# Where four short transposes stand in TensorE's order: among the projections, or behind the values of two blocks

## The chip, the cores and the metric

The kernel runs on one core of one Trainium2 chip. The time is device microseconds (us) from start to end of one execution; of several runs the median counts. An execution recorded by the hardware profiler gives the trace from which all durations here are taken.

## What is computed

Two transformer blocks, one after the other, work in float32 on `x` of 8 batches, 512 tokens and width 256. The change touches block 0 alone. Cut to its core it is:

```python
def _L0_xcond_ref(x, c, brain_tokens, ...):           # H = 16 heads of width 16
    h = modulate(ln(x), shift_sa, scale_sa)
    q = ln(_heads(h, H)) * qn_w + qn_b
    k = ln(_heads(h, H)) * kn_w + kn_b
    v = _heads(h, H)
    attn = softmax(einsum('bhqd,bhkd->bhqk', q, k) * scale)
    x = x + gate_sa * _unheads(einsum('bhqk,bhkd->bhqd', attn, v))
    h = modulate(ln(x), shift_ca, scale_ca)           # cross-attention over 64 context tokens
    ...
    x = x + gate_ca * h
    h = modulate(ln(x), shift_ff, scale_ff)
    h = silu(h @ w1.T) * (h @ w3.T) @ w2.T
    return x + gate_ff * h
```

Block 1 (self-attention with rotary positions, cross-attention, a GELU layer) follows with heads of width 64.

## The kernel before, in words

**Blocks of scores and values.** Self-attention of a batch is cut into four head groups `g` of four heads, and each into four key tiles `kt` of 128 keys: sixteen blocks. A block's scores are four matmuls with 16 rows each, which share the array (`block`, L577), into two of the two-bank PSUM tiles `ps_S` (there are two of these in all); then ACT takes the exponential of both halves (L590). A block's values are four matmuls of 32 columns into `ps_O` (L596). Cross-attention of a batch is two further blocks (L693), whose values also hold the matmuls of the denominators.

**Everything else** is hung beside the blocks by number with `at(i, fn)`, a plain list for each block number. A batch has a cycle of 18 numbers (`CYCLE`), of which 16 are its own blocks and two, 11 and 13, hold the cross-attention blocks of the batch before. Three stages run at once, each a cycle later: self-attention of batch b (`batch1`), cross-attention of b − 1 (`batch2`), feed-forward of b − 2 (`batch3`). What hangs beside the blocks are the projections (queries of cross-attention L684 to L691, `up` L766, `down` L783, `project_out` L454, and in the second cycle `keys1` L857, eight early projections for block 1), the norms, and the short transposes: sets of four 128x128 transposes into one PSUM bank.

- `queries_keys(g)` (L564): one set (L570), evacuated by ACT into `q` (L573) and by DVE into `k` (L574).
- `group_back(g)` (L606): one set of the attention's result `oT` (L610), then DVE (L617 to L620), then POOL adds it to `x` (L621, L622). `group_end` (L601) had copied `ps_O` to `oT` on ACT.
- `turn` of `batch2` (L683) and of `batch3` (L764): two sets each (`transposed`, L421, its transposes L427), evacuated by ACT (L428).

**The order.** All instructions of TensorE, VectorE (DVE), ScalarE (ACT) and GpSimd (POOL) are issued in the order in which the functions are called; nothing reorders them. `run_blocks` (L52) gives that order. Up to block 18 it goes block by block. After that it takes two blocks at a time: scores of the first, everything that hangs beside (for two numbers), scores of the second, values of two blocks. Such a pass over two blocks is called a group here, by its first block: group 41 has the scores of 41, the work hung at 39 and 40, the scores of 42, and the values of 40 and 41.

**PSUM.** Transposes, projections and cross-attention's values take their bank from `bank_x` (L106), which hands out three banks in turn: two of `ps_X` and `ps_D`. A bank that is handed out again has to wait for the reader of its former content, for `up` that is the DVE instruction L780 or L781.

Of the kernel before, what the change touches and what calls it, by code (L numbers as in the profile page):

```python
# [17 lines left out]
B, N, D, H, T, CD, FF = 8, 512, 256, 16, 64, 192, 1024  # L18
# [30 lines left out]
        self.scores, self.values = scores, values  # L49


def run_blocks(blocks, beside, alone):  # L52

    def scores(i):
        for fn in blocks[i].scores if i < len(blocks) else []:
            fn()

    def values(i):
        for fn in blocks[i].values if 0 <= i < len(blocks) else []:
            fn()

    def others(i):
        for fn in beside.get(i, []):
            fn()

    others(-1)
    for i in range(alone):  # L70
        scores(i)
        values(i - 1)
        others(i)
    scores(alone)
    values(alone - 1)
    for i in range(alone + 1, max(len(blocks) + 2, *(k + 3 for k in beside)), 2):
        scores(i)
        if i > alone + 1:
            others(i - 2)
        others(i - 1)  # L80
        scores(i + 1)
        values(i - 1)
        values(i)


def fast_path(ctx: ExitStack, tc: tile.TileContext, a: dict, out: bass.AP):
# [394 lines left out]


    blocks = []
    beside = {}

    def at(i, fn):
        beside.setdefault(max(i, -1), []).append(fn)

    CYCLE = H + 2
    X0, X1 = 11, 13  # L490
# [2 lines left out]
    def batch1(b):  # L493
        s = {}
        base = CYCLE * b
# [68 lines left out]
        def queries_keys(g):  # L564

            c, par = divmod(g, 2)
            ps = bank_x()
            lo = par * HD0
            for t in range(NT):
                nc.tensor.transpose(ps[:, t * P : (t + 1) * P], zs[c][:, t, lo : lo + P], ident)  # L570
            q = wk.tile([P, N], F32, tag="q", name="q", bufs=2)
            k = wk.tile([P, N], F32, tag="k", name="k", bufs=2)
            nc.scalar.activation(q, ps, AF.Identity, bias=qk_cols[:, 1:2], scale=qk_cols[:, 0:1])  # L573
            nc.vector.tensor_scalar(k, ps, col("kw"), col("kb"), ALU.mult, ALU.add)  # L574
            s[g] = (q, k)
# [30 lines left out]
        def group_back(g):  # L606
            c, par = divmod(g, 2)
            ps = bank_x()
            for t in range(NT):
                nc.tensor.transpose(ps[:, t * P : (t + 1) * P], s["oT", g][:, t * P : (t + 1) * P], ident)  # L610
            attn = wk.tile([P, NT, 4, HD0], F32, tag="attn", name="attn", bufs=1)
            x, gate = (v.rearrange("p t (h d) -> p t h d", d=HD0)[:, :, 8 * c + par : 8 * c + 8 : 2]
                       for v in (xs[b], s["gate"][:, None, :]))
            i = ps.rearrange("p (t j e) -> p t j e", t=NT, j=4)
            inv = small.tile([P, NT, 4], F32, tag="inv", name="inv")
            den = small.tile([P, NT, 4], F32, tag="den", name="den")
            nc.vector.tensor_copy(den, i[:, :, :, HD0])  # L617
            nc.vector.reciprocal(inv, den)
            nc.vector.tensor_tensor(attn, i[:, :, :, 0:HD0], inv[:, :, :, None].to_broadcast([P, NT, 4, HD0]), ALU.mult)  # L619
            check(inv.rearrange("p t j -> p (t j)"))  # L620
            nc.gpsimd.tensor_tensor(attn, attn, gate.to_broadcast([P, NT, 4, HD0]), ALU.mult)  # L621
            nc.gpsimd.tensor_tensor(x, x, attn, ALU.add)  # L622

        n = 0
        for g in range(4):
            for kt in range(NT):
                while n in (X0, X1):
                    n += 1
                i = base + n
                blocks[i] = block(g, kt)  # L630
                if g == 0 and kt == 0:
                    if b == 0:
                        def before():
                            for n in range(3):
                                norm(n)
                            nc.vector.tensor_copy(qk_cols, cols[:, 0:2])
                            for fn in (first_modulated, head_centre, head_square, head_var):
                                fn(0, 0)
                            head_scale(0, 0, nc.vector)

                        at(-1, before)
                        at(0, lambda: awake(3))
                        for k, par, fns in ((0, 1, (first_modulated, head_centre)),
                                            (1, 1, (head_square, head_var, head_scale)), (2, None, (first_modulated,)),
                                            (3, None, (head_centre,)), (4, None, (head_square, head_var, head_scale))):
                            for fn in fns:
                                at(k, lambda fn=fn, par=par: fn(0 if par else 1, par))
                        at(5, lambda: spread(s["gate"], b, G_SA, D))
                    else:

                        for m, k in enumerate((-11, -10, -9) if b == 1 else (-13, -12, -10)):
                            at(i + k, lambda m=m: norm(m))
                        for c in range(2):
                            for k, fn in zip((-6, -5, -5, -4) if b == 1 else (-7, -5, -3, -3) if c else (-9, -8, -7, -7),
                                             (head_centre, head_square, head_var, head_scale)):
                                at(i + k, lambda c=c, fn=fn: fn(c))
                if kt == 0:
                    at(i - (2 if i <= CYCLE else 4), lambda g=g: queries_keys(g))
                if kt == NT - 1:
                    at(i + 1, lambda g=g: group_end(g))  # L660
                    at(i + 2 + (b > 0 and n % 2 == 0), lambda g=g: group_back(g))
                n += 1


    def batch2(b):
        s = {}
        base = CYCLE * (b + 1)
# [67 lines left out]

        for n, i in enumerate((2, 2, 3)):
            at(base + i, lambda n=n: prepare(n))
        at(base + 5, turn)
        at(base + 7, lambda: queries(0))
        at(base + 8, lambda: queries(1))  # L740
        end = b == B - 1
# [9 lines left out]
    def batch3(b):  # L751
        s = {}

        base = CYCLE * (b + 2) + {B - 3: 4, B - 2: 3, B - 1: -2}.get(b, 0)

        def prepare(n):

            if n == 0:
                s["gate"] = gate = wk3.tile([P, D], F32, tag="gate3", name="gate3")
                spread(gate, b, G_FF, D)  # L760
                s["pieces"] = normed_in_pieces(wk2, b, EPS0, lambda z: s.update(z=z))
            s["pieces"][n]()

        def turn():  # L764
            s["hT"] = transposed(wk2, s["z"], b, modT[:, 6:8, :], modT[:, 4:6, :])

        def up(f):
            if f == 0:
                s["hid"] = wk3.tile([P, 8, N], F32, tag="hid", name="hid", bufs=1)
            fs = slice(f * P, (f + 1) * P)  # L770
            pss = []
            for w in (w_1, w_3):
                ps = bank_x()
                for k in range(2):
                    mm(ps, w[:, k, fs], s["hT"][:, k, :], k == 0, k == 1)
                pss.append(ps)

            t = wk3.tile([P, N], F32, tag="t", name="t")
            nc.scalar.activation(t, pss[0], AF.Tanh, scale=0.5)
            nc.vector.scalar_tensor_tensor(t, t, 1.0, pss[0], ALU.add, ALU.mult)  # L780
            nc.vector.tensor_tensor(s["hid"][:, f, :], pss[1], t, ALU.mult)  # L781

        def down(t):  # L783
            ps = bank_x()[:, 0:D]
            project_tile(ps, 0, lambda k: s["hid"][:, k, :], w_2, 8, t)
            tmp = wk2.tile([P, 2, D], F32, tag="tmp", name="tmp", bufs=1)[:, 0, :]
            nc.vector.tensor_tensor(tmp, ps, s["gate"], ALU.mult)
            x = xs[b][:, t, :]
            nc.vector.tensor_tensor(x, x, tmp, ALU.add)

        places = {B - 2: (3, 3, 5, 6, 8), B - 1: (2, 2, 2, 4, 7)}.get(b, (4, 4, 6, 8, 9))
        for n in range(3):
            at(base + places[n], lambda n=n: prepare(n))
        later.append((base + places[3], turn))
        for f in range(8):
            at(base + places[4] + f, lambda f=f: up(f))
        for t in range(4):
            at(base + places[4] + 8 + (t if b > B - 3 else 2 * t), lambda t=t: down(t))

    blocks = [Block([], []) for _ in range(CYCLE * (B + 2))]  # L800
# [120 lines left out]
    later = []  # L921
    for b in range(B):
        batch2(b)
        batch3(b)
    for i, fn in later:
        at(i, fn)
    run_blocks(blocks, beside, CYCLE)
    ms.close()
    l0.close()

# [1334 lines left out]
```

## Time and profile before

| | us |
|---|---|
| median of three runs | 2419.1 |
| lowest and highest | 2417.03, 2423.43 |
| the profiled execution | 2413.9 |
| its span, first to last instruction | 2411.8 |
| block 0 in it, until the first projection of block 1's keys | 838.4 |

In a row of the timeline the first number is the start from the beginning of the span, the second the time until the last end of the merged instructions; then engine, line, operation, tiles as out<-in, the rows and columns of the array and the shape, how many instructions, and the idle time before them with what ended it. Matmuls overlap, and all matmuls of the kernel are issued by one helper, so they carry its line, L116; the transposes carry their own. In the view by stretches each engine has its busy time, and at the end of the row stand the granted share of TensorE's clock, the share of the DMA engines and GB/s. In the chain of work each share is the part of the span for which that engine's work was what the end waited for.

### The profile page before, as it was taken

The numbers are of one execution on the slowest core, as the hardware profiler recorded it, in microseconds if no ns is written. First come the engines' busy times: TensorE is split into PE (matmuls) and PEld (weight loads), VectorE is DVE, ScalarE is ACT, GpSimd is POOL, SyncE is SP. The second block draws the span as 40 slices with busy tenths as digits, with TensorE's granted clock in tenths as the row PEclk, the third lists the DMA queues.
The fourth block names the chain that finished last, engine by engine and source line by source line (L and its number), as shares of the span: only waits on it lengthen the run. The fifth ranks groups of instructions, "written<-read, shape, count | busy, mean of one in ns | idle before, by whom it ended". The sixth has DMA issues, their size and how long they took to land.

```text
span 2411.8 us, 28553 instructions
## 1 busy us (share of the span) xinstructions
PE 2379.0 (99%) x10964; PEld 1158.8 (48%) x10964; DVE 1139.5 (47%) x2115; ACT 889.2 (37%) x1118; POOL 966.5 (40%) x588
## 2 busy tenths in 40 slices
PE   9999999999999999999999999999999999999998
PEld 4333544544545633434343444444445556567665
DVE  4564534434345344555454555545445656651110
ACT  4665545545442134333333333333342212221221
POOL 4563323323201046555555554646453445441110
PEclk9999999999999999999999999999999999999999
DMA  5130000000002001000101010100023212210000
GB/s 184 33 107 11 16 15 13 16 14 6 12 11 92 0 1 32 14 24 10 28 10 28 10 28 10 28 10 26 30 67 95 77 58 68 64 56 31 18 22 20
DMA packets 84897, 84.07 MB, mean 35 GB/s; under 512 B 42656, under 2 KB 59792, under 8 KB 84752
## 3 DMA queue, kind: packets, MB, share of 16 engines
q1 hardware_dynamic: 83208, 78.99, 11.0%
q8 instruction: 88, 1.44, 0.2%
q0 software_dynamic: 640, 2.10, 0.2%
q10 hardware_dynamic: 904, 1.07, 0.2%
q14 instruction: 57, 0.47, 0.1%
HBM read 72.09 MB, written 10.04 MB: 34 GB/s over the span
## 4 chain that ended last, share of the span: by engine, by line
PE 87%; DVE 4%; POOL 3%; issue 3%; DMA 1%; ACT 1%; SPq 1%; POOLq 0%; DVEq 0%; ACTq 0%
PE ps_X L116 36%; PE ps_S L116 22%; PE ps_D L116 13%; PE ps_O L116 13%; PE ps_X L427 1%; DMA rb<-rec 1%; DVE t L843 1%; POOL x L448 1%; DVE sm L1039 1%; POOL p L1277 1%; ACT p L590 0%; PE ps_X L610 0%; POOL var L561 0%; DVE t L1000 0%; SPq L1270 0%
## 5 line engine op out<-in xcount | busy, mean ns | idle before, releaser
L116 PE MATMUL ps_S<-q,k 32*128 32x512 f32 (+1 forms) x3072 | 425.6, 623 | 5.5 <-ACT p L590 3.4
L1020 ACT ACTIVATE p<-ps_S 128x1024 f32<-128x1024 f32 x256 | 250.8, 1022 | 459.7 <-PE ps_S L116 450.3
L590 ACT ACTIVATE p<-ps_S 128x1024 f32<-128x1024 f32 x256 | 248.3, 1022 | 171.6 <-PE ps_S L116 170.3
L116 PEld LDWEIGHTS ps_S<-q,k 32*128 32x128 f32 (+1 forms) x3072 | 148.7, 183 | 244.8 <-issue 155.5
L1039 DVE TENSOR_TENSOR sm<-sm,p 128x1024 f32<-128x1024 f32 x128 | 252.1, 2028 | 0.1
L999 DVE TENSOR_TENSOR t<-ps_X,rope_c 128x512 f32<-128x512 f32 x126 | 87.0, 690 | 341.0 <-PE ps_X L116 341.0
L1002 POOL TENSOR_TENSOR q<-t 128x512 f32<-128x512 f32 x32 | 65.5, 2047 | 294.3 <-DVE t L1000 294.3
L182 POOL TENSOR_TENSOR rstd<-rstd,mhalf 128x4 f32<-128x4 f32 x49 | 51.2, 1044 | 293.6 <-DVE rstd L181 292.6
L844 POOL TENSOR_TENSOR q<-t,t 128x512 f32<-128x512 f32 x72 | 94.9, 1319 | 172.6 <-DVE t L843 171.6
L116 PE MATMUL ps_X<-hT,w 128*128 128x512 f32 x328 | 151.0, 597 | 0.5 <-DVE t L780 0.5
L1035 POOL TENSOR_TENSOR sm<-p 128x1024 f32<-128x1024 f32 x64 | 149.7, 2364 | 1.9 <-ACT p L1020 1.9
L1085 POOL TENSOR_TENSOR oT<-oT,rb 128x512 f32<-128x512 f32 x63 | 128.9, 2065 | 19.6 <-DMA rb<-rec_d 19.6
L116 PE MATMUL ps_O<-p,v 128*64 128x512 f32 x512 | 134.9, 605 | 0.0
L116 PE MATMUL ps_D<-p,v 128*64 128x512 f32 x512 | 131.6, 592 | 0.0
L116 PE MATMUL ps_O<-p,h 128*32 128x512 f32 x1024 | 129.5, 609 | 0.6 <-ACT p L590 0.6
L621 POOL TENSOR_TENSOR attn<-attn,gate 128x256 f32<-128x256 f32 x32 | 23.3, 727 | 250.7 <-DVE attn L619 250.7
L116 PE MATMUL ps_X<-w_sa_wv,hT 128*128 128x512 f32 x256 | 118.0, 604 | 0.0
L1002 POOL TENSOR_TENSOR k<-t 128x512 f32<-128x512 f32 x32 | 40.7, 1272 | 192.8 <-DVE t L1000 192.8
L116 PE MATMUL ps_X<-hT,w_sa_wq 128*128 128x512 f32 x256 | 115.9, 595 | 0.0
L116 PE MATMUL ps_X<-w_sa_wo,oT 128*128 128x256 f32 x512 | 114.5, 382 | 0.1
L116 PE MATMUL ps_X<-hT,w_sa_wk 128*128 128x512 f32 x248 | 114.6, 605 | 0.0
L116 PE MATMUL ps_S<-hT,w_ff_w 128*128 128x512 f32 x256 | 111.3, 593 | 0.0
(286 smaller groups left out, 3663.6 us busy)
## 6 DMA issues: line engine op xcount, KB each, us to landing
rb<-rec SPq DMA_DIRECT2D x128, 128.0 KB
rb<-rec_d SPq DMA_DIRECT2D x124, 128.0 KB
rb<-rec SPq DMA_DIRECT2D x16, 256.0 KB
out_dram<-x SPq DMA_DIRECT2D x15, 256.0 KB
x<-in_x_dram SPq DMA_DIRECT2D x7, 512.0 KB
gate<-modd SPq DMA_DIRECT2D x24, 128.0 KB
k_d<-q POOLq DMA_DIRECT2D x8, 256.0 KB, 2.4
v_d<-v SPq DMA_DIRECT2D x8, 256.0 KB
```

Source lines behind the costliest of these rows:

```text
L116: nc.tensor.matmul(o, lhsT, rhs, start=start, stop=stop)
L182: nc.gpsimd.tensor_tensor(r[:, :n], r[:, :n], mhalf[:, :n], ALU.pow)
L427: nc.tensor.transpose(ps[:, t * P : (t + 1) * P], z[:, t, k * P : (k + 1) * P], ident)
L448: nc.gpsimd.tensor_tensor(xs[b], xs[b], r[:, None, :].to_broadcast([P, NT, D]), ALU.add)
L590: nc.scalar.activation(pr[u], pss[u], AF.Exp, scale=HD0 ** -0.5)
L844: nc.gpsimd.tensor_tensor(dst, t1, t2, ALU.add)
L999: nc.vector.tensor_tensor(c, ps, rope_c, ALU.mult)
L1002: nc.gpsimd.tensor_tensor(r[0], ec, os, ALU.subtract)
L1020: nc.scalar.activation(pr, pss[u], AF.Exp, scale=HD1 ** -0.5)
L1035: nc.gpsimd.tensor_tensor(sm, s["p", g, 0, u], s["p", g, 1, u], ALU.add)
L1039: nc.vector.tensor_tensor(s["sm", g, u], s["sm", g, u], s["p", g, t, u], ALU.add)
L1085: eng.tensor_tensor(o, o, s["rb", g, u], ALU.mult)
```

## The change

A second list, `behind`, is added to `beside`. What hangs in it is called at the end of a group, after the values of its two blocks and in front of the next group's scores. A new helper `then` puts a function there, or, for numbers below 17, into the old list. The sets of four transposes use it: `queries_keys`, `group_back`, `turn` of `batch2`, and `turn` of `batch3` for all batches but the last two. Some numbers are changed with it: `group_back` goes to the first number after its group's last block (to the fourth for g = 2), `turn` of `batch2` one number later (for the last batch one earlier), and the third preparation of `batch3` one number later.

```diff
-def run_blocks(blocks, beside, alone):
+def run_blocks(blocks, beside, behind, alone):
...
-    for i in range(alone + 1, max(len(blocks) + 2, *(k + 3 for k in beside)), 2):
+    for i in range(alone + 1, max(len(blocks) + 2, *(k + 3 for k in (*beside, *behind))), 2):
         scores(i)
         if i > alone + 1:
             others(i - 2)
         others(i - 1)
         scores(i + 1)
         values(i - 1)
         values(i)
+        for fn in (*behind.get(i - 2, []), *behind.get(i - 1, [])):
+            fn()
...
+    def then(i, fn):
+        (beside if i < CYCLE - 1 else behind).setdefault(max(i, -1), []).append(fn)
...
                 if kt == 0:
-                    at(i - (2 if i <= CYCLE else 4), lambda g=g: queries_keys(g))
+                    then(i - (2 if i <= CYCLE else 4), lambda g=g: queries_keys(g))
                 if kt == NT - 1:
                     at(i + 1, lambda g=g: group_end(g))
-                    at(i + 2 + (b > 0 and n % 2 == 0), lambda g=g: group_back(g))
+                    then(i + (2 if i + 2 < CYCLE else 4 if g == 2 else 1), lambda g=g: group_back(g))
...
-        at(base + 5, turn)
+        then(base + (4 if b == B - 1 else 6), turn)
...
-        places = {B - 2: (3, 3, 5, 6, 8), B - 1: (2, 2, 2, 4, 7)}.get(b, (4, 4, 6, 8, 9))
+        places = {B - 2: (3, 3, 5, 6, 8), B - 1: (2, 2, 2, 4, 7)}.get(b, (4, 4, 7, 8, 9))
...
-        later.append((base + places[3], turn))
+        later.append((at if b > B - 3 else then, base + places[3], turn))
...
-    for i, fn in later:
-        at(i, fn)
-    run_blocks(blocks, beside, CYCLE)
+    for put, i, fn in later:
+        put(i, fn)
+    run_blocks(blocks, beside, behind, CYCLE)
```

More of the change, by code (lines that the diff above doesn't have):

```diff
@@ L483, in fast_path @@
     blocks = []
-    beside = {}
+    beside, behind = {}, {}
     def at(i, fn):
         beside.setdefault(max(i, -1), []).append(fn)
+    def then(i, fn):
+        (beside if i < CYCLE - 1 else behind).setdefault(max(i, -1), []).append(fn)
     CYCLE = H + 2
```

## The prediction

> **What bounds the kernel now.** I read the page first: engine shares and the chain of work.
>
> ```profile
> PE 2379.0 (99%) x10964; PEld 1158.8 (48%) x10964; DVE 1139.5 (47%) x2115; ACT 889.2 (37%) x1118; POOL 966.5 (40%) x588
> PE 87%; DVE 4%; POOL 3%; issue 3%; DMA 1%; ACT 1%; SPq 1%; POOLq 0%; DVEq 0%; ACTq 0%
> ```
>
> TensorE sets the time. Block 0 takes the first 838 us; its share of busy is no help, because a matmul's end is modelled. So I read the timeline, and took every duration as start of one row to start of the next. A float32 matmul leaves two records, a transpose one. This is group 87 and the start of 89, then the exps on ACT:
>
> ```profile
> 407.95 1.98 PE L116 MATMUL ps_X<-hT,w 128*128 128x512 f32 x4
> 409.78 1.88 PE L116 MATMUL ps_D<-hT,w 128*128 128x512 f32 x4
> 411.49 0.60 PE L570 MATMUL ps_X<-ident,z 128*128 128x128 f32 x4
> 412.26 1.98 PE L116 MATMUL ps_X<-hT,w 128*128 128x512 f32 x4 [0.17 <-DVE t L780]
> 414.08 1.88 PE L116 MATMUL ps_D<-hT,w 128*128 128x512 f32 x4
> 415.89 1.14 PE L116 MATMUL ps_S<-q,k 16*128 16x512 f32 x8
> 416.96 1.92 PE L116 MATMUL ps_O<-p,h 128*32 128x512 f32 x16
> 418.82 1.43 PE L116 MATMUL ps_S<-q,k 16*128 16x512 f32 x8
> 420.17 0.66 PE L610 MATMUL ps_X<-ident,oT 128*128 128x128 f32 x4
> 420.67 1.88 PE L116 MATMUL ps_X<-hT,w 128*128 128x512 f32 x4
> ...
> 417.13 1.94 ACT L590 ACTIVATE p<-ps_S 128x1024 f32<-128x1024 f32 x2 [2.25 <-PE ps_S L116]
> 420.05 1.94 ACT L590 ACTIVATE p<-ps_S 128x1024 f32<-128x1024 f32 x2 [0.99 <-PE ps_S L116]
> ```
>
> Scores at 415.89 take 1.07 us, the next at 418.82 take 1.36. No idle is booked, but their second PSUM pair comes free only when the exps end (417.13 + 1.94 = 419.07): scores want 3.23 us from one start to the next, and values of two blocks give 2.93. That is a hidden stall of 0.29 per group. Second, a set of four transposes between two projections costs more than its 0.44: at 411.49 it takes the third bank, the next projection waits for DVE's L780, 0.77 to its start.
>
> Sets behind values exist in batch 0, and one kind of group has no projections at all (group 41):
>
> ```profile
> 43.33 1.07 PE L116 MATMUL ps_O<-p,h 128*32 128x512 f32 x8
> 44.32 0.66 PE L570 MATMUL ps_X<-ident,z 128*128 128x128 f32 x4
> 44.91 1.27 PE L116 MATMUL ps_S<-q,k 16*128 16x512 f32 x6
> ...
> 170.16 1.43 PE L116 MATMUL ps_S<-q,k 16*128 16x512 f32 x8
> 171.51 0.66 PE L570 MATMUL ps_X<-ident,z 128*128 128x128 f32 x4
> 172.47 2.04 PE L116 MATMUL ps_S<-q,k 16*128 16x512 f32 x8 [0.30 <-ACT p L590]
> 174.44 1.92 PE L116 MATMUL ps_O<-p,h 128*32 128x512 f32 x16
> ```
>
> Behind values the set costs 0.59 (44.32 to 44.91). In group 41 both scores take 4.28 us together (170.16 to 174.44), bound by ACT; the set between them is free. Last, the clock by stretches:
>
> ```profile
> 154.88:158.30 3.42, 3.12 (x20) 1.07 (x14) 0.60 (x4) 2.73 (x4) 3.34 (x2) 1.00 0.07 8
> 158.30:161.71 3.41, 3.41 (x18) 0.60 (x16) 1.50 (x2) 2.19 (x3) 3.38 (x5) 0.50 0.45 160
> ```
>
> The third column from the right is the granted clock. Group 37 has the same work as 41, but took 7.78 us instead of 6.14: after a stretch that held only 16-row scores and transposes the clock was halved. That dip cost 1.64 us.
>
> [...] the first projection behind scores takes 0.53 instead of 0.43, and a set behind scores or values 0.06 more at its first transpose and 0.09 more before the next scores. [...]
>
> **The change, part by part.** All arithmetic and DMAs stay; 84 sets of four transposes move (29 of attention back, 27 of queries and keys, 14 pairs of turns). No moved step issues a DMA, so no queue is passed. Prices, us:
> - Removed: a set ahead of scores or of another set 0.44 (435.47 to 436.00 is 0.53, 0.09 of it the change to scores, which stays). Attention back directly behind scores 0.39 (0.49, but the projection then pays the 0.10). Queries and keys between two projections 0.61 in one group of a batch (0.50, and 0.10 for weights that came late), 0.87 in the next (0.77 and 0.10).
> - Added: 0.59 for the first set behind values, 0.44 for each further; minus 0.29 where the scores that follow stalled.
> - A group left with one projection of keys (1.91 us) starts its second scores 2.99 after the first; 3.23 are wanted: +0.23.
> - A group left with nothing: 0 for what goes, full price for what comes.
>
> "Next scores" are sped by a set only if they aren't the first of a group of that last kind (there the 4.28 counts from their start) and if no cross block was among the values (2.71, no stall).
>
> By group (its first block), order written down from the loops:
> - A batch in steady state, 55 to 71: 55 −0.44+1.02−0.29 = +0.30; 57 −0.39; 59 +0.30; 61 −0.39−0.87+1.02−0.29 = −0.53; 63 −0.87+1.46−0.29 = +0.30; 65 −0.39−0.61+0.59 = −0.41; 67 0; 69 −0.87+0.59−0.29 = −0.57; 71 −0.39+0.59−0.29 = −0.09. Sum −1.09; four such batches −4.36.
> - 45 to 53, like 63 to 71: −0.77.
> - Opening: 19 +1.02 (nothing left), 21 0, 23 −0.39+0.23+1.02−0.29 = +0.57, 25 −0.39−0.87+0.23+1.02−0.29 = −0.30, 27 +0.30, 29 −0.39−0.44+0.59 = −0.24, 31 0, 33 −0.57 (the set waited 0.64 for POOL's L562, which is over by then; −0.39−0.64+0.16+0.59−0.29), 35 −0.39+0.23+0.59 = +0.43, 37 +1.02, 39 −0.39, 41 +1.02, 43 +1.02−0.24 = +0.78. Sum +3.64.
> - End: 127 +0.30, 129 −0.39, 131 +0.30, 133 −0.53, 135 +0.59, 137 +0.59, 139 +1.02, later 0 (sets among projections only). Sum +1.88.
>
> Total 3.64 − 0.77 − 4.36 + 1.88 = +0.4 us. What steady batches win, the groups emptied of their cover give back.
>
> Costed at nothing: the evacuations. Four transposes issued at t end at about t+0.7; ACT's copy (0.78, L573) ends at t+1.5, the next exp can't start before t+0.59+1.24 = t+1.83. With two or three sets the last copies end about 0.3 ahead of the exp. Were this cover gone, exps would slip by some 0.3 per group, into projections of 3.4 us and more. DVE (L574, L617 to L619) ends its projections' work 2.9 us before the sets. Attention back comes one group earlier for three of four, so the later norms wait less for POOL. batch3's third preparation comes one group later, 5 us or more ahead of its turn. Bank rotation: between a projection and a set lie scores and values, 2.9 us, more than any evacuation.
>
> Unknown is the clock. Five pairs of 16-row scores, 4.28 us long, can hold a whole window (19, 21, 37, 41, 43); this trace has one dip in them. After the change none has transposes within. Zero dips is −1.6, five +6.6 beside today's one. I take one, as now.
>
> Profiled execution: 2413.9 us (span 2411.8 and 2.1 around it); the sum gives 2414.3. The median of the runs is 2419.1, 5.2 above; the same +0.4 there is 2419.5.
>
> **The rivals.**
> - *Stall not filled (slower).* The bank wait moves along with the sets, because their evacuation on ACT delays the exps. Then the 34 credits of 0.29 and the 0.24 fall away: +10.1, 2429.6. For it: ACT is in order, the copy stands between two exps. Against: the gaps worked out above, and free banks after long spacing (1.07 at 415.89). It decides from about 0.20 us lost in each of 34 groups.
> - *Clock.* Three or more dips: +3.7 to +7.0, 2423 to 2426.
> - [...] if a set in between costs 0.44 instead of 0.59, 48 places win 7.2: 2412. Against: 0.59 at 44.32 and 29.26.
> - *Less waiting elsewhere.* Waits like group 33's end in more places, no dip: 2413 to 2417.
>
> **How the numbers follow.** Likeliest 0.67: 2419.5, own range 2415 to 2424. Stall not filled 0.10, clock 0.08, [...] less waiting 0.09. 0.3% is 7.3 us, about what a measurement can tell: faster lies under 2411.8, slower above 2426.4. Range 2411 to 2428: it leaves out most of the first rival and little below. Faster 0.07 [...], slower 0.13 (the stall and part of the clock), same 0.80.
>
> **What would show it.** Per steady batch 94.2 us in place of 95.3 (239.96 to 335.26 now). Scores behind a moved set 1.07, never 1.36. Sixteen projection records of L775 (recorded as L116) in one stretch of 7.06, without a wait for L780. Groups 19, 37, 41 at 7.16. Wrong if scores behind sets keep 1.36, if a set behind values takes over 0.65, if L573 or L428 delays an exp, or if the clock is at half in several stretches between 88 and 183 us.

## The result

The changed kernel takes 2431.5 us (median of 6 runs, 2429.5 to 2432.6); the kernel before 2421.1 in the same comparison. The ratio is 1.0047, with a 95% interval of 1.0034 to 1.0061: slower by some 10 us, outside the predicted range of 2411 to 2428. The profiled execution took 2431.5 (span 2429.6), that of before 2413.9.

The page after, engine shares and the chain of work. All lines of the code stand 2 to 6 further down than before (L118 for L116, L576 for L570, L616 for L610, L429 for L427):

```profile
PE 2389.2 (98%) x10964; PEld 1153.6 (47%) x10964; DVE 1142.0 (47%) x2115; ACT 890.0 (37%) x1118; POOL 966.7 (40%) x588
PE 88%; DVE 5%; issue 3%; POOL 2%; DMA 1%; ACT 1%; SPq 0%; POOLq 0%; DVEq 0%; ACTq 0%
```

The bound is the same, and nothing here tells where 17.8 us of span went. The timeline of TensorE does. First the end of group 87 and the start of 89, as shown of before:

```profile
421.44 1.98 PE L118 MATMUL ps_X<-hT,w 128*128 128x512 f32 x4
423.26 1.88 PE L118 MATMUL ps_D<-hT,w 128*128 128x512 f32 x4
424.98 3.60 PE L118 MATMUL ps_X<-hT,w 128*128 128x512 f32 x8
428.51 1.14 PE L118 MATMUL ps_S<-q,k 16*128 16x512 f32 x8
429.58 1.92 PE L118 MATMUL ps_O<-p,h 128*32 128x512 f32 x16
431.43 0.66 PE L576 MATMUL ps_D<-ident,z 128*128 128x128 f32 x4
432.02 1.14 PE L118 MATMUL ps_S<-q,k 16*128 16x512 f32 x8
433.09 3.70 PE L118 MATMUL ps_X<-hT,w 128*128 128x512 f32 x8
```

From 421.44 to 428.51 the projections take 7.07 us without a break: the wait for L780 is gone. The set behind the values costs 0.59 (431.43 to 432.02), and the scores behind it 1.07 instead of 1.36. The loss isn't here. Group 41, a pair of scores with nothing left between:

```profile
179.39 1.43 PE L118 MATMUL ps_S<-q,k 16*128 16x512 f32 x8
181.70 2.04 PE L118 MATMUL ps_S<-q,k 16*128 16x512 f32 x8 [0.88 <-ACT p L596]
183.67 3.10 PE L118 MATMUL ps_O<-p,h 128*32 128x512 f32 x16
186.70 1.12 PE L616 MATMUL ps_X<-ident,oT 128*128 128x128 f32 x4
187.61 0.65 PE L576 MATMUL ps_D<-ident,z 128*128 128x128 f32 x4
188.18 1.14 PE L118 MATMUL ps_S<-q,k 16*128 16x512 f32 x8
```

Before, the scores of group 43 followed the values of this group at 176.29:

```profile
174.44 1.92 PE L116 MATMUL ps_O<-p,h 128*32 128x512 f32 x16
176.29 1.20 PE L116 MATMUL ps_S<-q,k 16*128 16x512 f32 x8
```

The pair takes 4.28 (179.39 to 183.67), as before; but the values then take 3.03 instead of 1.85, and the first of the two sets behind them 0.91, where it takes 0.49 at full clock (114.79 to 115.28, in group 23). The view by stretches, for groups 19, 21, 41 and 43, has the granted clock in the third column from the right:

```profile
88.96:99.34 10.38, 9.78 (x44) 3.41 (x40) 0.39 (x2) 4.99 (x6) 0.00 (x0) 0.67 0.36 90
99.34:108.15 8.81, 7.64 (x34) 1.72 (x33) 5.20 (x18) 4.76 (x5) 4.68 (x5) 0.67 0.04 15
179.39:188.18 8.79, 7.91 (x44) 3.02 (x40) 5.10 (x19) 4.51 (x6) 5.13 (x4) 0.81 0.53 172
188.18:198.45 10.27, 9.10 (x41) 3.01 (x40) 3.42 (x14) 5.09 (x6) 2.47 (x3) 0.67 0.01 2
```

In each of these groups a stretch at half clock (0.50) of 3.4 or 6.8 us begins; that of group 21 ends in group 23. Set against the kernel before, group by group from one first score to the next (us):

| groups | predicted | measured | half-clock time before, after |
|---|---|---|---|
| 19 | +1.02 | +4.25 | 0, 6.8 |
| 21 and 23 | +0.57 | +4.03 | 0, 6.8 |
| 25 to 35 | −0.38 | −0.15 | none |
| 37 | +1.02 | +1.07 | 3.4, 3.4 |
| 39 | −0.39 | −0.39 | none |
| 41 and 43 | +1.80 | +6.79 | 0, 10.2 |
| 45 to 53 | −0.77 | −0.73 | none |
| a batch, 55 to 71 and three more | −1.09 | −1.09 each | none |
| 127 to 135 | +0.27 | −0.02 | none |
| 137 | +0.59 | +2.29 | 0, 3.4 |
| 139 | +1.02 | +1.03 | none |
| 143 to 153 | 0 | +4.29 | 0, 3.4 |

(Measured differences carry the 0.29 of a stall in the group of the stalled scores, the prediction in the group of the set; so neighbours shift by 0.29.) What is left of the 17.8 is +0.5 ahead of the first scores, +0.4 near the end of block 0 and −1.2 in block 1; these weren't followed up.

The last row holds a second loss. The turn of the last batch, one group earlier than before:

```profile
739.14 1.78 DVE L217 TENSOR_SCALAR z<-x,mv,rstd 128x256 f32<-128x256 f32 x4
740.01 1.44 PE L429 MATMUL ps_D<-ident,z 128*128 128x128 f32 x4 [1.94 <-DVE z L217]
```

TensorE waits 1.94 us for the norm of the last batch, then takes its four tiles as they come, 0.32 apart; a half-clock stretch begins at the third of them. Before, the same two sets stood behind one more `down`, and waited for nothing:

```profile
723.69 3.62 PE L116 MATMUL ps_D<-w,hid 128*128 128x256 f32 x16
727.14 1.04 PE L427 MATMUL ps_X<-ident,z 128*128 128x128 f32 x8
```

### The profile page after: what moved, and what is told of

Its sections match the earlier page's. It is cut to its first block, busy times and chain, and to the rows that moved or that the text cites. A ratio compares the mean times of both kernels' runs of the same rounds, so it can differ in the third digit from the quotient of the medians.

```text
span 2429.6 us, 28557 instructions
## 1 busy us (share of the span) xinstructions
PE 2389.2 (98%) x10964; PEld 1153.6 (47%) x10964; DVE 1142.0 (47%) x2115; ACT 890.0 (37%) x1118; POOL 966.7 (40%) x588
## 3 DMA queue, kind: packets, MB, share of 16 engines
q10 hardware_dynamic: 904, 1.07, 0.1%
## 4 chain that ended last, share of the span: by engine, by line
PE 88%; DVE 5%; issue 3%; POOL 2%; DMA 1%; ACT 1%; SPq 0%; POOLq 0%; DVEq 0%; ACTq 0%
PE ps_X L118 36%; PE ps_S L118 22%; PE ps_D L118 14%; PE ps_O L118 14%; PE ps_X L429 1%; DVE sm L1045 1%; DMA rb<-rec 1%; DVE t L849 1%; POOL p L1283 1%; PE ps_X L616 1%; DVE t L1006 0%; POOL var L567 0%; PE ps_X L576 0%; DVE z L217 0%; DVE t L846 0%
## 5 line engine op out<-in xcount | busy, mean ns | idle before, releaser
L118 PE MATMUL ps_S<-q,k 32*128 32x512 f32 (+1 forms) x3072 | 420.6, 625 | 11.5 <-ACT p L596 7.2
L118 PEld LDWEIGHTS ps_S<-q,k 32*128 32x128 f32 (+1 forms) x3072 | 141.7, 184 | 238.8 <-issue 166.6
L567 POOL TENSOR_TENSOR var<-var,mhalf 128x32 f32<-128x32 f32 (+1 forms) x17 | 87.3, 5137 | 175.9 <-DVE var L561 175.9
L118 PE MATMUL ps_X<-hT,w 128*128 128x512 f32 x328 | 150.5, 597 | 0.0
L118 PE MATMUL ps_O<-p,h 128*32 128x512 f32 x1024 | 135.6, 635 | 0.6 <-ACT p L596 0.6
L118 PE MATMUL ps_O<-p,v 128*64 128x512 f32 x512 | 134.9, 605 | 0.0
L118 PE MATMUL ps_D<-p,v 128*64 128x512 f32 x512 | 131.6, 592 | 0.0
L118 PE MATMUL ps_X<-w_sa_wv,hT 128*128 128x512 f32 x256 | 118.0, 604 | 0.0
L118 PE MATMUL ps_X<-hT,w_sa_wq 128*128 128x512 f32 x256 | 115.9, 595 | 0.0
L118 PE MATMUL ps_X<-w_sa_wo,oT 128*128 128x256 f32 x512 | 114.5, 382 | 0.1
L118 PE MATMUL ps_X<-hT,w_sa_wk 128*128 128x512 f32 x248 | 114.6, 605 | 0.0
L118 PE MATMUL ps_S<-hT,w_ff_w 128*128 128x512 f32 x256 | 111.3, 593 | 0.0
```

Of the source, the lines that this page charges most:

```text
L118: nc.tensor.matmul(o, lhsT, rhs, start=start, stop=stop)
L567: nc.gpsimd.tensor_tensor(var, var, half, ALU.pow)
```

## The experiments

Two theories of the clock were set against each other and against waits: A, a set between two scores keeps the clock up, and its removal lets it fall; B, a set there does nothing for the clock, and the sets behind the values lengthen the lull ahead of the next pair. Both were the author's guesses; the trace of before had one stretch among these pairs to go by. Every run has its granted clock on record, and the time follows it: over the 110 runs of the kernel before, the time falls by 2.4 us for each 0.001 that the clock rises, a thousandth of the time itself. So time × (1 − clock) is taken as what is lost to the clock. The last column of the table is the median of the times less that loss. The clock is recorded to 0.001, so that column is good to about 1 us, no better. Each ratio is to the runs of the kernel before in the same comparison.

| kernel | runs | median us | ratio to before, 95% interval | mean clock | at full clock |
|---|---|---|---|---|---|
| before | 110 | 2419.7 | | 0.9960 | 2409.5 |
| changed | 6 | 2431.5 | 1.0047 (1.0034 to 1.0061) | 0.9920 | 2412.1 |
| changed, matmuls between the emptied pairs | 20 | 2418.6 | 1.0010 (0.9998 to 1.0021) | 0.9967 | 2412.7 |
| changed, sets between the emptied pairs | 20 | 2424.6 | 1.0020 (1.0011 to 1.0030) | 0.9952 | 2412.8 |
| before, empty sets behind values | 20 | 2422.5 | 1.0021 (1.0011 to 1.0030) | 0.9956 | 2412.8 |
| before, one matmul in four pairs | 10 | 2415.2 | 0.9980 (0.9967 to 0.9993) | 0.9971 | 2409.0 |
| selective | 8 | 2412.4 | 0.9974 (0.9958 to 0.9990) | 0.9961 | 2405.0 |
| changed, last turn back | 16 | 2428.8 | 1.0039 (1.0029 to 1.0049) | 0.9922 | 2409.4 |
| selective, one matmul in four pairs | 14 | 2408.4 | 0.9960 (0.9948 to 0.9972) | 0.9979 | 2404.3 |
| before, four pairs emptied | 20 | 2423.8 | 1.0020 (1.0008 to 1.0032) | 0.9940 | 2410.6 |

**Matmuls between the emptied pairs.**

```diff
+    def cover(n):
+        ps = bank_x()
+        for _ in range(n):
+            mm(ps[:, 0:D], ident, w_o0[:, 0, :])
+    for i in (18, 20, 36, 40, 42, 136, 138):
+        at(i, lambda: cover(2))
```

> The changed kernel, with two matmuls of 128 rows and 256 columns put between the two scores of groups 19, 21, 37, 41, 43, 137 and 139, which the change left without any work there (about 1.05 us of TensorE in a gap of 1.24; their result is not read). Clock theory (the emptied pairs leave TensorE so idle that the clock is halved): the half-clock stretches in these groups go (11 windows of 3.4 us before block 1 become about 3), granted clock 0.992 to about 0.997, time about 2417. Rival (the time was lost to waits for the exps or for other engines in these groups): nothing gained, 2431 or up to 2 us more.

Measured 2418.6. The stretches of groups 19 and 21, and one that lies 0.2 us later than group 37:

```profile
88.42:95.58 7.16, 7.16 (x48) 3.16 (x44) 0.29 (x2) 4.89 (x6) 0.00 (x0) 1.00 0.56 130
95.58:101.72 6.14, 6.03 (x37) 2.01 (x37) 4.18 (x15) 4.65 (x5) 3.17 (x4) 1.00 0.07 21
156.13:163.29 7.16, 7.05 (x48) 2.87 (x48) 1.72 (x8) 4.35 (x6) 6.52 (x8) 1.00 0.30 105
```

More work in the gap, 13 us less time. Groups 19 and 21 take 7.16 and 6.14, as the sum had them, at full clock. So the loss in the pairs is the clock and no wait: a wait would have stayed. The median is 1.6 above the expectation: a third of the runs lie near 2426 at a clock of 0.994 to 0.995, with stretches that this profile doesn't hold.

**Sets between the emptied pairs.** The same with `nc.tensor.transpose(ps[:, t * P : (t + 1) * P], ident, ident)` four times instead of the matmuls, once per pair.

> The changed kernel, with one set of four transposes of the identity (result not read) between the two scores of the same seven groups, where the kernel before had its own sets. Theory A (a set between two scores counts as activity, and its removal let the clock fall): the half-clock stretches go as with matmuls, about 2418 to 2421. Theory B ([...] the sets that now stand behind the values lengthen the lull before the next pair): the stretches stay, 2431.

Measured 2424.6, clock 0.9952. Neither number was met: sets between bring back 7 of the 13 us. So a set between two scores helps to keep the clock (0.9952 against 0.9920). That it does less than the two matmuls says little about transposes: a set fills 0.5 us of the gap, the two matmuls 1.06.

**Empty sets behind values.**

```diff
+        for fn in behind.get(i, []):
+            fn()
...
+    def empty_set():
+        ps = bank_x()
+        for t in range(NT):
+            nc.tensor.transpose(ps[:, t * P : (t + 1) * P], ident, ident)
...
+    behind = {19: [empty_set] * 2, 35: [empty_set], 37: [empty_set] * 2, 41: [empty_set] * 2, 43: [empty_set] * 2}
```

> The kernel before, with empty sets of four transposes (of the identity, not read) added behind the values of groups 19 (two), 35 (one), 37, 41 and 43 (two each), as many as the change puts there. Their price by the sum is 4.7 us, less 0.3 where group 45's scores had stalled. Theory A: the clock is as in the kernel before, 2425.5. Theory B: more half-clock stretches in groups 21, 37 and 43, 2430 or more.

Measured 2422.5, below both numbers, with a clock of 0.9956 against 0.9960. The sets cost about their price (+3.3 at full clock, 4.4 by the sum). The clock is lower by 0.0004, with a standard error of 0.0003; the change lowers it by 0.0040. So B alone doesn't account for the loss. (The one profile here has three stretches after block 18, in groups 21, 37 and 41, where that of before has one; its clock of 0.996 is that of a usual run of before.)

**Four pairs emptied in the kernel before.**

```diff
-                    at(i - (2 if i <= CYCLE else 4), lambda g=g: queries_keys(g))
+                    early = {(1, 1): 17, (2, 1): 34, (2, 2): 38}.get((b, g))
+                    at(early or i - (2 if i <= CYCLE else 4), lambda g=g: queries_keys(g))
...
-                    at(i + 2 + (b > 0 and n % 2 == 0), lambda g=g: group_back(g))
+                    at(21 if (b, g) == (0, 3) else i + 2 + (b > 0 and n % 2 == 0), lambda g=g: group_back(g))
```

> The kernel before, with the single sets of groups 19, 21, 37 and 41 moved among the projections of a neighbouring group (queries and keys of groups 1,1 and 2,1 and 2,2 earlier, attention back 0,3 later). These four pairs are left empty, and no set stands behind values. By the prices +1.7 us, 2421.4. Theory A (a set between two scores keeps the clock up): more half-clock stretches in 19, 21, 37 and 41, clock 0.994 or less, 2425 to 2428. Theory B (only sets behind the values lower it): 0.996, 2421.4.

Measured 2423.8, clock 0.9940, +1.1 at full clock. Groups 19 and 21 of its profile, in stretches that begin 0.2 to 0.3 us after the groups:

```profile
88.80:96.20 7.40, 7.13 (x36) 1.74 (x38) 1.66 (x9) 4.89 (x6) 1.01 (x1) 0.81 0.51 129
96.20:104.50 8.30, 7.12 (x36) 1.75 (x40) 0.00 (x0) 3.98 (x4) 0.00 (x0) 0.76 0.00 0
```

Removal alone, with nothing behind the values, lowers the clock: 0.0020 less (standard error 0.0004), 4.8 us of 2420. The time stays 1.2 below the low end of A's expectation. The loss of clock is half of the change's 0.0040; the change empties three pairs more, two of which (43 and 137) had three half-clock windows in its profile, 0.0021 of the span. Whether sets behind an emptied pair add something of their own is not settled.

**One matmul in four pairs of the kernel before** (`cover(1)` at 18, 20, 36, 40).

> The kernel before, with one matmul of 128 rows and 256 columns (result not read) behind the set that stands between the two scores of groups 19, 21, 37 and 41. Clock theory: the profiled execution of the kernel before had one half-clock stretch there and took 2413.9, its median is 2421; if the 7 us are further such stretches, they all go: about 2412.5, with little spread. Rival (the spread of the kernel before has another source): 2420 to 2421.

Measured 2415.2, 4.5 us faster than before, and at full clock the same (2409.0 and 2409.5): a gain by the clock alone. The expectation was too good: three of the ten runs remain at 0.995. Where their stretches lie, no trace shows.

**Last turn back.**

```diff
-        then(base + (4 if b == B - 1 else 6), turn)
+        if b == B - 1:
+            at(base + 5, turn)
+        else:
+            then(base + 6, turn)
```

> The changed kernel, with the turn of the last batch of batch2 alone back in the place of the kernel before (one group later, among the projections). If the wait of its first set for DVE's z (2.7 us in group 149, with one half-clock stretch of 1.6 behind it) is what its earlier place costs: 2427 to 2428.8. If the wait only moves to the later place: 2431.5.

Measured 2428.8, the upper end of the expectation: 2.7 less than the changed kernel at an equal clock (0.9922 and 0.9920). The intervals of the two ratios overlap, so the trace has to decide:

```profile
737.76 3.62 PE L118 MATMUL ps_D<-w,hid 128*128 128x256 f32 x16
741.21 1.04 PE L429 MATMUL ps_X<-ident,z 128*128 128x128 f32 x8
```

No wait for L217 is left there, and groups 143 to 153 are 4.29 shorter than in the changed kernel, of which 1.7 is the half-clock stretch. At full clock the change is then level with before, which fits its sum of +0.4 within the 1 us of that column.

**Selective.** The sets that would leave a pair empty, attention back of groups 35 and 39 and of the last batch's last two head groups, and the last turn keep their old places; the others stand behind the values.

```diff
+                    put = at if (b, g) in ((1, 1), (2, 1), (2, 2), (7, 3)) else then
+                    put(i - (2 if i <= CYCLE else 4), lambda g=g: queries_keys(g))
...
+                    if (b, g) in ((0, 3), (1, 2), (1, 3), (2, 0), (7, 1), (7, 2), (7, 3)):
+                        at(i + 2 + (b > 0 and n % 2 == 0), lambda g=g: group_back(g))
...
+        if b in (1, B - 1):
+            at(base + 5, turn)
+        else:
+            then(base + 6, turn)
```

The turn of `batch3` for batch 5, with its third preparation, keeps its place as well.

> The changed kernel, but the sets that would leave a pair of scores with nothing between (groups 19, 21, 37, 41, 43, 137, 139), attention back of group 35 and the turn of the last batch keep the places of the kernel before; all other sets stand behind the values. By the prices: opening +0.3, 45 to 53 -0.7, four batches -4.4, end -0.3, together -5.1 us. Clock theory: the granted clock is as in the kernel before (about 0.996), time about 2414.5, ratio 0.998. Rival (sets behind values lower the clock too): 0.995 or less, 2418 and more.

> The selective kernel, with one matmul of 128 rows and 256 columns (result not read) behind the set in groups 19, 21, 37 and 41, as in the kernel before with that matmul (2415.2). The prices say 5.1 us less than that: 2410, ratio to the kernel before 0.996. If the half-clock stretches come back elsewhere: 2414 or more.

Measured 2412.4 and, with the matmul, 2408.4. At full clock 4.5 and 5.2 below before, where the prices said 5.1. Both beat both kernels; the second by 0.4% (0.9948 to 0.9972). In the selective kernel the sets behind values leave the clock where it was (0.9961 in 8 runs, standard error 0.0005).

## Why the prediction was wrong

**Right: the prices.** Away from the half-clock stretches the sum came out almost group by group: −1.09 per steady batch (94.21 us), 7.16 for an emptied group at full clock, 1.07 for scores behind a set, 7.07 for the projections. Two emptied pairs that met no half-clock stretch show it without any matmul put in: in the profile of the kernel with its last turn back, group 21 takes 6.14 and group 41 7.16. The 0.10 by which the first projection behind scores is longer (0.53 for 0.43) is the one price whose cause stays open: at 412.26, behind a set and a wait, it takes 0.53 as well. The rival "stall not filled" is refuted by the scores in the timeline, the one in which a set behind values costs 0.44 (2412, put at 0.06) by the 0.59 of each set. The total of +0.4 is what the kernel with its last turn back shows at full clock (2409.4 against 2409.5, to about 1 us).

**Wrong: "I take one, as now".** This step of the sum, the clock, failed. It kept the number of half-clock stretches at one, without a reason, though the prediction had written down that the five pairs lose the transposes that stood between. The mean clock fell from 0.9960 to 0.9920, 9.7 us of 2420; nearly all of the measured difference. The rival "Clock" was the right one, and its sign of being wrong, the clock at half in several stretches from 88 us on, is what the profile shows; but it had 8% and was mis-sized: it counted 16-row pairs and one window each. The profile has six pairs with a stretch, the sixth (137) beginning with 32-row scores, and three of them last two windows.

**Wrong: one execution as the base.** The profile of before held one stretch after block 18; its 110 runs spread over 14 us, at clocks of 0.994 to 0.998. The prediction took the 5.2 us between profile and median as an offset without a cause. Most of it is the clock in these pairs: one matmul in four of them takes 4.5 us off the median and nothing off the time at full clock. The spread told how easily these pairs lose the clock.

**Wrong: "later 0".** The turn of the last batch was costed as a move among projections. One group earlier it stands ahead of its own norm: 1.94 us of wait, tiles that come one by one and a half-clock stretch, 4.29 us in the traces and 2.7 in the medians.

**Mis-sized: group 29**, −0.01 instead of −0.24, or −0.53 with the 0.29 that the set ahead of it saves there: its set waited 0.5 for a bank that the rotary multiplications of the keys (L849 of the changed kernel) still read. "More than any evacuation" was too wide a claim; with two key projections ahead DVE was late.

## What to carry to other kernels

A gap in the bounding engine that costs nothing in the sum may still be worth its filling (13 us here, by matmuls that nobody reads): ask what a move leaves behind in the place that it leaves, and whether the clock holds there. Before a forecast, compare the granted clock of several runs (0.994 to 0.998 here), not of the profiled one alone (0.998); in this kernel, which TensorE bounds, time × (1 − clock) separates schedule from clock to about 1 us. And where a schedule change wins in the steady state, look at the lead-in and the tail by themselves: here their groups have too little other work to cover the pair, and the same idea, applied only where cover remains, gained 0.3% (0.1 to 0.4).

## What was not expected of the hardware

The clock fell after windows in which TensorE's array was far from idle: before group 37's stretch the view shows 3.12 of 3.42 us busy, with 16-row matmuls and transposes (the ends of matmuls are modelled, so the busy share may be too high). So the fall came behind a window that held work, but little of it in projections and values.

How little, the ten traces together tell. In both kernels' profiles the granted clock changes only at whole multiples of 3.41 us from its first change in block 0 (72.96 us into the span before, 75.06 after). Cut the time from 20 to 205 us into windows of this length and place, and add up in each TensorE's work other than scores (projections, values, transposes), every instruction until the next one starts, 0.44 us at most. Of the windows at full clock, all 25 with 0.90 us or less of this were followed by one at half clock, 5 of 33 with 0.91 to 1.25, and none of 436 with more. Group 37 of before had 0.82 in such a window, group 41 1.31: the same work, cut differently: the one window begins 0.54 us behind the first score of its group (154.88), the other 1.79 (171.95). In the changed kernel the windows ahead of the stretches in its emptied pairs up to group 43 had 0.05 to 0.61. This is a reading after the fact, of one kernel and its variants; no run tested it.

Transposes help to keep the clock up: one set between two scores brought the changed kernel from 0.9920 to 0.9952, and the windows can be told apart with transposes counted like other work. Whether they do less for it than matmuls isn't settled: between 0.91 and 1.25, four of the five windows that a half-clock one followed held some, and six of the 28 others.

And a stretch can last: in the profile of the kernel with its last turn back the clock stayed at half for 20.5 us, from block 16 on, where little but scores, values and transposes runs. The other nine profiles have a stretch of one or two windows near there, between 73 and 80 us. What decides between one window and six isn't settled. Five more windows cost 8.5 us (1.7 each), about what the third of runs near 2426 with matmuls in the pairs lose; whether that is their cause no trace shows.
